# A second level of Strassen's block products in a fused attention block: q, k and the projection with 49 products in place of 56, their weights streamed from DRAM

## The chip, the cores and the metric

One Trainium2 chip, one of its cores. The metric is the device time of one launch in microseconds (us). A kernel is run several times; the median is quoted. Ratios and their 95% intervals are computed from fast runs against runs of the kernel before in the same rounds on the same chip. Every run used here is fast, with a mean granted TensorE clock between 0.988 and 0.999 of full.

Names of engines in the profile: PE is TensorE's matmuls, PEld its weight loads, DVE is VectorE, ACT is ScalarE, POOL is GpSimd, SP is SyncE, which issues most transfers here. SBUF is the memory on the core, PSUM the banks in which TensorE accumulates.

## The reference, cut to what matters

For each of 16 images of 512 channels and 32 x 32 = 1024 positions, in fp32: group normalisation, attention with 4 heads of 128 channels, a projection, and the residual.

```python
def _L0_conv_ref(x, norm_gamma, norm_beta, qkv_w, qkv_b, proj_w, proj_b):
    xg = x.reshape(b, NUM_GROUPS, -1)                      # b = 16, NUM_GROUPS = 8
    xn = ((xg - mu) * jax.lax.rsqrt(var + EPS)).reshape(b, c, h, w)
    xn = xn * norm_gamma[:, None, None] + norm_beta[:, None, None]
    qkv = jnp.einsum('oc,bchw->bohw', qkv_w, xn) + qkv_b[:, None, None]
    q, k, v = jnp.split(qkv, 3, axis=1)                    # then to 4 heads
    attn = jax.nn.softmax(jnp.einsum('bhnd,bhmd->bhnm', q, k) * scale, axis=-1)
    out = jnp.einsum('bhnm,bhmd->bhnd', attn, v)           # back to b, c, h, w
    out = jnp.einsum('oc,bchw->bohw', proj_w, out) + proj_b[:, None, None]
    return x + out
```

## The kernel before

It already uses one level of Strassen's scheme (in Winograd's form, with few additions): the q/k, v and projection products are cut into 2 x 2 blocks, and 7 block products replace 8. TensorE does the seven; the sums of weight blocks (`s1` to `s4`) are made once; the sums of data blocks (`t1` to `t4`) and the recombination of the seven results are made for each image, most of them on VectorE.

```python
FACTORS = {     # product: (weight block or sum, data block or sum)
    1: ("a11", "b11"), 2: ("a12", "b21"), 3: ("s4", "b22"), 4: ("a22", "t4"),
    5: ("s1", "t1"), 6: ("s2", "t2"), 7: ("s3", "t3"),
}

def quad(name, mm, results, order=(1, 6, 2, 7, 5, 4, 3), home=None):
    # bank(i): one of TWO PSUM banks that rotate under one tag
    def p1():
        mm(bank(1), 1, True)
        u["p1"] = upool.tile(...)
        nc.scalar.copy(u["p1"], banks[1])
    def p6():
        mm(bank(6), 6, True)
        nc.vector.tensor_add(u[2], banks[6], u["p1"])
    def p2():
        mm(banks[1], 2, False)           # accumulates onto product 1
        results["c11"](banks[1])
    ...                                  # p7, p5, p4, p3 in the same way

# q/k of one head: mm is two matmuls (k = 0, 1) of 512 columns
# projection, residual and bias; `eng` is GpSimd here, res[...] holds x:
def add(u, *places):
    for at in places:
        eng.tensor_add(res[at], res[at], u)         # both inputs in SBUF
def put(which, half):
    ...
    nc.vector.scalar_tensor_tensor(t, acc, bias, t, ALU.add, ALU.add)   # acc in PSUM
```

Attention runs in 512 steps (16 images x 4 heads x 8 blocks of 128 positions). In each, TensorE makes a block of scores (two matmuls of 512 columns in the program, 4 instructions in the trace: 2048 over the 512 steps), ScalarE its exponentials `p`, VectorE adds them to `tot`, and TensorE the weighted sum of the step before into `po`. Products are spread over the steps as "units", issued between a step's scores and the weighted sum:

```python
for s in range(steps + 1):
    if s < steps:
        b, h, j = where(s)
        if j == 0:
            plan = plan_head(b, h)       # which products run beside this head
        scores(s)
        if j == 2 and s > NB:
            divide(*where(s - NB)[:2])
        for u in plan[j]:
            u()
    if s > 0:
        if s % NB == 0:
            denominators(*where(s - 1)[:2])
        weighted_sum(s - 1)              # po: one PSUM tile; ScalarE copies it to o after 8
```

The compiler then orders the instructions of each engine.

## Time and profile before

| | before |
|---|---|
| time, median of the fast runs | 3372.2 us |
| first to last `tot` transpose (64, one per head), "the stretch" | 3234.7 us |
| from the last of them to the end | 38.4 us |
| one image in the steady state (mean of images 1 to 14) | 208.3 us |
| of this, TensorE not streaming columns | 2.1 us |

The stretch is read from the source view of the transposes, which gives the first and the last start. It is one line per kernel:

```profile
L491 DVE STREAM_TRANSPOSE tt<-tot x64: 1232/1236/1246, 95.7 to 3330.4; 128x1024 f32<-128x1024 f32 x64
```

The last row of the table is a count of mine over the trace: start of each matmul to start of the next, less the time that its columns take at the constant rate that the prediction reads (0.429 us for 512 columns, half of it for 256). Recounts from the packed traces give 1.9 to 2.3 us here, according to how narrow matmuls are priced, so differences of a few tenths in such counts mean little. I use the count because the page's busy share hides losses: ends of matmuls are modelled. A matmul alone is recorded with 0.38 us where its 256 columns take 0.216, and a gap inside a group counts as busy. The rest of the profile before is in the prediction.

### The profile page before, as it was taken

To read this page: it belongs to the slowest core of one execution; us is meant where nothing else is said; L and a number is where in the kernel's file an instruction comes from. 1 tells how busy PE (TensorE), PEld (TensorE's weight loads), DVE (VectorE), ACT (ScalarE), POOL (GpSimd) and SP (SyncE) were. 2 spreads that over 40 slices of the span, in tenths; PEclk is the share of its full clock that TensorE was granted. 3 is DMA by queue.
4 is the path that set the end of the run, shared out by engine and by line. 5 is a ranking of instruction groups with operands and counts; after the bars stand their busy time and mean duration, and the time that the engine had idled before them with its cause. 6 is when DMAs were issued, how large, how long until landed. Compare 5 with 4: busy or idle time off the path is not lost. (4 is left out here: it accounts for less than half of the span.)

```text
span 3368.8 us, 23014 instructions
## 1 busy us (share of the span) xinstructions
PE 3334.8 (99%) x8692; PEld 1634.4 (49%) x8692; DVE 1632.5 (48%) x2454; ACT 790.7 (23%) x870; POOL 141.9 (4%) x110
## 2 busy tenths in 40 slices
PE   8999999999999999999999999999999999999998
PEld 5454454544545445454544545445454454544543
DVE  5553544535445364544545445454454534545444
ACT  2221212212222122221222222221222212222121
POOL 0000000000000000000000000000000000000000
PEclk9999999999999999999999999999999999999999
DMA  2101111011110111101111010110101101011011
GB/s 75 38 21 48 38 41 53 25 44 38 46 48 26 44 38 50 44 25 44 38 53 41 25 50 32 53 41 26 50 31 57 38 25 50 32 60 41 25 44 63
DMA packets 63813, 140.25 MB, mean 42 GB/s; under 512 B 10448, under 2 KB 14544, under 8 KB 63696
## 3 DMA queue, kind: packets, MB, share of 16 engines
q1 hardware_dynamic: 62688, 137.66, 12.0%
q8 instruction: 70, 1.15, 0.1%
q10 hardware_dynamic: 1008, 1.06, 0.1%
q14 instruction: 47, 0.39, 0.0%
HBM read 104.87 MB, written 33.82 MB: 41 GB/s over the span
## 5 line engine op out<-in xcount | busy, mean ns | idle before, releaser
L479 ACT ACTIVATE p<-s 128x1024 f32<-128x1024 f32 x512 | 522.6, 1024 | 2054.3 <-PE s L474 2049.6
L518 PE MATMUL po<-p,v 128*128 128x512 f32 x2048 | 976.5, 594 | 0.0
L474 PE MATMUL s<-qk,qk 128*128 128x512 f32 x2048 | 962.3, 592 | 0.0
L484 DVE TENSOR_TENSOR tot<-tot,p 128x1024 f32<-128x1024 f32 x384 | 470.1, 1224 | 920.5 <-ACT p L479 920.0
L474 PEld LDWEIGHTS s<-qk,qk 128*128 128x128 f32 x2048 | 389.1, 190 | 489.4 <-issue 474.8
L518 PEld LDWEIGHTS po<-p,v 128*128 128x128 f32 x2048 | 385.4, 190 | 453.5 <-issue 393.0
L351 PE MATMUL qk<-xt,wqk_a 128*128 128x512 f32 x512 | 242.5, 596 | 6.3 <-DVE qk_u L315 5.5
L351 PE MATMUL qk<-x,wqk_s 128*128 128x512 f32 x512 | 243.3, 593 | 2.2 <-DVE qk L368 2.2
L351 PE MATMUL qk<-x,wqk_a 128*128 128x512 f32 x512 | 242.2, 595 | 0.0
L527 DVE TENSOR_TENSOR o<-o,rinv 128x1024 f32<-128x1024 f32 x64 | 78.4, 1225 | 244.5 <-ACT o L524 128.7
L439 POOL TENSOR_TENSOR y<-y,pp_u 128x512 f32<-128x512 f32 x90 | 112.7, 1266 | 1882.6 <-DVE pp_u L315 1758.5
L351 PEld LDWEIGHTS qk<-xt,wqk_a 128*128 128x128 f32 x512 | 95.9, 190 | 133.9 <-issue 114.1
L351 PEld LDWEIGHTS qk<-x,wqk_s 128*128 128x128 f32 x512 | 97.0, 190 | 125.8 <-issue 116.1
L351 PEld LDWEIGHTS qk<-x,wqk_a 128*128 128x128 f32 x512 | 95.9, 190 | 126.7 <-issue 106.7
L445 DVE SCALAR_TENSOR_TENSOR y<-pp,projb_sb,y 128x512 f32<-128x512 f32 x124 | 92.7, 748 | 120.6 <-PE pp L418 99.8
L368 DVE SCALAR_TENSOR_TENSOR qk<-qk,qkb_sb,qk_u 128x512 f32<-128x512 f32 x192 | 142.0, 746 | 11.5 <-PE qk L351 11.4
L351 PE MATMUL qk<-xt,wqk_s 128*128 128x512 f32 x256 | 120.6, 593 | 2.0 <-DMA wqk_a<-in_qkv_wT 2.0
L384 PE MATMUL v<-wv_a,xt 128*128 128x256 f32 x512 | 120.9, 379 | 0.0
L384 PE MATMUL v<-wv_s,x 128*128 128x256 f32 x512 | 120.9, 379 | 0.0
L384 PE MATMUL v<-wv_a,x 128*128 128x256 f32 x512 | 120.9, 379 | 0.0
L418 PE MATMUL pp<-ot,wp_a 128*128 128x512 f32 x248 | 118.4, 599 | 0.8 <-DVE pp_u L325 0.8
L418 PE MATMUL pp<-o,wp_a 128*128 128x512 f32 x248 | 118.1, 598 | 1.0 <-DVE o L527 1.0
(104 smaller groups left out, 2062.7 us busy)
## 6 DMA issues: line engine op xcount, KB each, us to landing
rinv<-row SPq DMA_DIRECT2D x64, 512.0 KB, 3.6
y<-in_x SPq DMA_DIRECT2D x128, 256.0 KB, 2.8
out_y<-y SPq DMA_DIRECT2D x128, 256.0 KB, 2.0
x<-in_x SPq DMA_DIRECT2D x62, 512.0 KB, 3.8
wqk_a<-in_qkv_wT SPq DMA_DIRECT2D x8, 192.0 KB, 4.5
x<-in_x ACTq DMA_DIRECT2D x2, 512.0 KB, 6.8
wv_a<-in_qkv_wT SPq DMA_DIRECT2D x8, 128.0 KB, 2.9
wp_a<-in_proj_wT SPq DMA_DIRECT2D x8, 128.0 KB, 3.4
```

Of the source, the lines that this page charges most:

```text
L351: nc.tensor.matmul(acc, wqk[wn][k][:, ts(h, P)], xb[b][xn][k], start=(first and k == 0), stop=(k == KC - 1), skip_group_check=True,)
L368: return lambda acc, u: nc.vector.scalar_tensor_tensor(dst(which, half), acc, bias(which), u, ALU.add, ALU.add)
L384: nc.tensor.matmul(acc[:, ts(g, HC)], xb[b][xn][k][:, ts(2 * jj + g, P)], wv[wn][k], start=(first and g == 0 and k == 0), stop=(k == KC - ...
L418: nc.tensor.matmul(acc, wp[wn][k][:, ts(o, P)], ob[b][on][k], start=(first and k == 0), stop=(k == KC - 1), skip_group_check=True,)
L439: eng.tensor_add(res[at], res[at], u)
L445: nc.vector.scalar_tensor_tensor(t, acc, bias, t, ALU.add, ALU.add)
L474: nc.tensor.matmul(sc[:, ts(half, HALF)], ks[b, h][:, ts(j, P)], qs[b, h][:, ts(half, HALF)], start=True, stop=True,)
L479: nc.scalar.activation(ps[s], sc, AF.Exp, scale=SCALE)
L484: nc.vector.tensor_add(tot[b, h], tot[b, h], ps[s])
L518: nc.tensor.matmul(po[b, h][:, ts(half, HALF)], vs[b, h // 2][:, h % 2, j, :], p[:, ts(half, HALF)], start=(j == 0), stop=(j == NB - 1),)
L527: nc.vector.tensor_mul(os_[b, h], os_[b, h], rinv.pop((b, h)))
```

## The change

**Intent.** Apply the scheme a second time to each of the seven products of q and k (two heads at once, a "pair") and of the projection: 7 x 7 = 49 quarter-size products replace 7 x 8 = 56. TensorE has 12.5% fewer columns there. What it needs:

- Matmuls have 256 columns in place of 512, grouped so that two outer products share a bank's tile of 512 columns (`OUTER`).
- The weight sums of both levels are no longer held in SBUF. They are made for the first image, kept in DRAM, and streamed in 0.9 MB blocks, group by group.
- Each group needs inner data sums of 256 columns, evictions into `R`, and outer sums: all on VectorE and ScalarE.
- A group has one bank x and one bank y, in place of two banks that rotate.
- The normalisation of images 1 to 15 becomes two ScalarE passes; half of it was on VectorE.
- The residual adds of the projection stay on GpSimd: eight per image in place of six, one in front of each final add.

The core of the diff; the first launch's weight staging, the start, the end and the v part are cut:

```diff
+OUTER = ((1, 5), (2, 6), (7, 4), (3,))
+ORDER = (1, 2, 6, 5, 7, 4, 3)
...
-    ps_a = ctx.enter_context(tc.tile_pool(name="ps_a", bufs=2, space=bass.MemoryType.PSUM))
+    ps_a = ctx.enter_context(tc.tile_pool(name="ps_a", bufs=1, space=PSUM))
...
     def normalise(b, c, half=None):
         t = xs[b, c] if half is None else xs[b, c][:, ts(half, HALF)]
-        norm.apply(t, t, *scaled[b], c, True)
+        mu, sc, nmu = scaled[b]
+        if nmu is None:
+            norm.apply(t, t, mu, sc, c, True)
+        else:
+            i = slice(c, c + 1)
+            nc.scalar.activation(t, t, AF.Identity, bias=nmu[:, i])
+            nc.scalar.activation(t, t, AF.Identity, bias=beta_sb[:, i], scale=sc[:, i])
...
+    def group_weights(site, g, first):
+        group = OUTER[g]
+        w = wpool.tile([P, 2, 7, P], F32, tag="w", name=f"w_{site}_{g}")
+        if not first:
+            nc.sync.dma_start(w[:, : len(group)], store[site, g])
+            return w
...
+    def strassen(name, mm, out_, spare=False, width=HALF):
+        def bank(which):                      # which is "x" or "y"
+            return ps_a.tile([P, HALF], F32, tag=which, name=f"{name}_{which}")
+        def kept_copy(n):
+            nc.scalar.copy(t[n][:, :width], t["x"][:, :width])
+        def p1():
+            t["x"] = bank("x")
+            mm(t["x"], 1, True)
+            kept_copy("p1")
+        def p2():
+            t["y"] = bank("y")
+            mm(t["y"], 2, True)
+            out_("c11", t["y"], t["p1"])      # VectorE empties y
+        def p6():
+            mm(t["x"], 6, False)
+            kept_copy("u2")                   # ScalarE copies x
+        def p5():
+            t["y"] = bank("y")
+            mm(t["y"], 5, True)
...
+                for i, p in enumerate(group):        # the inner sums
+                    def put(o, a, c):
+                        nc.vector.tensor_sub(have[o][:, i, :], inner(i, a), inner(i, c))
+                    put("t1", "b12", "b11")
+                    put("t2", "b22", "t1")
+                    put("t3", "t2", "b11")
+                    put("t4", "b21", "t2")
...
+        def combine(g):                              # the outer sums
+            if g == 1:
+                finish("c11", part(0, 0), part(1, 0))
+                nc.vector.tensor_add(part(1, 1), part(0, 0), part(1, 1))
+                nc.vector.tensor_add(part(1, 0), part(1, 1), part(0, 1))
+            elif g == 2:
+                nc.vector.tensor_add(part(2, 0), part(1, 1), part(2, 0))
+                finish("c21", part(2, 0), part(2, 1))
+                finish("c22", part(2, 0), part(0, 1))
+            elif g == 3:
+                finish("c12", part(1, 0), part(3, 0))
...
+    def proj_groups(b, eng, **kw):
+        def finish(which, a, c):
+            for r in range(2):
+                ...                                  # t: residual x, loaded by DMA
+                eng.tensor_add(c[:, r, :], c[:, r, :], t)
+                nc.vector.scalar_tensor_tensor(
+                    t, a[:, r, :], projb_sb[:, o : o + 1], c[:, r, :], ALU.add, ALU.add
+                )
...
-            spread(plan, qk_units(b, 1), 0, NB)
+            spread(plan, sum(qk_groups(b, 1), []), 0, NB)
...
+                spread(plan, sum(proj_groups(b - 1, nc.gpsimd), []), 0, NB)
```

## The prediction

> **What bounds the kernel now.** I read the page first (busy shares, slices), then the groups by line, the timeline of single batches, and the chain that ended last.
>
> ```profile
> PE 3334.8 (99%) x8692; PEld 1634.4 (49%) x8692; DVE 1632.5 (48%) x2454; ACT 790.7 (23%) x870; POOL 141.9 (4%) x110
> PE   8999999999999999999999999999999999999998
> PEclk9999999999999999999999999999999999999999
> ```
> TensorE is busy 99% and its clock is full; no other engine passes half. Busy time alone does not prove that PE is at its own limit, so I read the spacing of matmuls in the timeline of one batch (start, length, work):
>
> ```profile
> 2930.36 1.88 PE L518 MATMUL po<-p,v 128*128 128x512 f32 x4
> 2932.07 1.88 PE L474 MATMUL s<-qk,qk 128*128 128x512 f32 x4
> 2933.79 1.89 PE L384 MATMUL v<-wv_a,x 128*128 128x256 f32 x8
> 2935.52 1.89 PE L384 MATMUL v<-wv_s,xt 128*128 128x256 f32 x8
> ```
> Starts are 1.71 to 1.73 us apart, whether the block is 4 instructions of 512 columns or 8 of 256: 0.429 us per 512 columns, 0.216 us per 256. So PE streams at a constant rate per column, and narrow matmuls cost nothing extra: the weight load (190 ns by its rows) hides behind a 216 ns matmul. Each fp32 matmul is two instructions. The end of the trace is a real chain: the last attention sum ends near 3331 us, the division waits for its denominators, and the projection follows.
>
> ```profile
> 3336.13 4.90 DMA rinv<-row
> 3341.13 1.24 DVE o L527
> ```
> Before kernel outside the steady state: PE starts at about 17 us and is the bound from about 21; after the last sum 37 us pass for 24 us of projection work. In between PE loses almost nothing (204.6 of 205 us busy between 1000 and 1205 us).
>
> [...] The change gives each group only one bank x and one bank y; no run yet shows what that costs. [...] Here 0.5 MB x loads land after 3.8 us[...].
>
> **The change, part by part.**
>
> *PE, removed.* Per batch, q and k have now 4 heads x 7 products x 2 halves of the contraction x 2 instructions = 112 of 512 columns (1792 over 16 batches, as counted): 112 x 0.4293 = 48.1 us. After: two pairs x 49 products x 2 instructions = 196 of 256 columns: 196 x 0.2159 = 42.3 us. The projection goes from 56 x 0.4293 = 24.0 to 98 x 0.2159 = 21.2 us. The v products stay one-level. Saved 5.8 + 2.9 = 8.6 us per batch, 138 us in 16. If all else hides: 3372 - 138 = **3234 us**, 4.1% less. That is the ceiling on the gain.
>
> *DVE, added.* The rows used:
>
> ```profile
> L315 DVE TENSOR_TENSOR qk_u<-qk,qk_p 128x512 f32<-128x512 f32 x64 | 43.3, 676 | 44.0 <-PE qk L351 44.0
> L368 DVE SCALAR_TENSOR_TENSOR qk<-qk,qkb_sb,qk_u 128x512 f32<-128x512 f32 x192 | 142.0, 746 | 11.5 <-PE qk L351 11.4
> L484 DVE TENSOR_TENSOR tot<-tot,p 128x1024 f32<-128x1024 f32 x384 | 470.1, 1224 | 920.5 <-ACT p L479 920.0
> L149 DVE TENSOR_TENSOR wv_s<-wv_s,wv_a 128x256 f32<-128x256 f32 x2 | 0.8, 414 | 0.0
> L310 ACT COPY qk_p<-qk 128x512 f32<-128x512 f32 x64 | 37.5, 586 | 83.0 <-PE qk L351 83.0
> ```
> One two-level site (a pair's q and k, or one projection) needs 7 x 4 inner sums of 256 columns, 28 x 0.414 = 11.6 us; 9 evictions of 512 columns and 3 of 256, 9 x 0.69 + 3 x 0.42 = 7.5; 3 outer adds of 1024 columns, 3.7; and, for q and k, 8 final adds with bias, 8 x 0.746 = 6.0. So 28.8 us per pair, 22.8 for the projection (its 8 final adds exist already): 80.4 us per batch, 1286 us in all, and perhaps 16 net for the weight sums done once. Removed: the u2 and u3 adds (175.7 us), the q/k bias adds (142.0) and the normalisation's DVE half for 15 batches (44.8): 362. DVE goes from 1632 to about **2570 us, 79% of the span**. Back to back, DVE instructions start closer together than they last (two 512-column sums in 1.28 us on the timeline, 1.21 us from one such pair to the next), so real room is larger than it looks.
>
> By head: PE needs 27.5 us of attention plus 21.2 us of units, 48.7 us (51 in the v head); DVE needs 13.6 for attention sums, denominators and division. Head 0 (28.8 + 13.6 + 5.4 for sums of o) is 47.8, head 1 (22.8 + 6.0 + 13.6 + 7.3 for statistics) 49.7, head 2 23, head 3 42.4. With the back-to-back rate, heads 0 and 1 come to some 42 to 44: close to PE, below it.
>
> *ACT.* Four copies per group in place of one per quad, 8.6 us per site at 586 ns and less for the short group, 4.7 for v; normalisation becomes two passes, 8 x 1.09 us in one burst at the end of head 1. From 791 to about 1210 us, 37%.
>
> *Banks.* A group is p1,p2,p6,p5,p7,p4,p3, of 0.86 us each. Bank x must be copied out by ACT (0.59 us and some 0.3 us of signalling on both sides, as read off the timeline) between p1,p6,p7,p4; bank y by DVE between p2,p5,p3. The other bank's product covers most of it: unbroken, a group takes about 7.2 us for 6.05 us of work, and 6.9 us of attention per group lies free to fill the gaps. The compiler's order does fill gaps already: where the sums of x delay q/k at the start of head 3, it pulls two blocks of scores together, and PE loses one small gap:
>
> ```profile
> 2889.95 3.60 PE L474 MATMUL s<-qk,qk 128*128 128x512 f32 x8
> 2901.86 1.98 PE L351 MATMUL qk<-xt,wqk_a 128*128 128x512 f32 x4 [0.36 <-DVE qk_u L315]
> ```
> Not every gap will be filled: outer adds and next inner sums form DVE bursts of 6 to 7 us between groups, and the ACT burst of 8.7 us holds exponentials and copies together. **I choose 2.4 us lost per batch, 36 us**; that is judged, not computed: about 0.2 us for each of 12 to 14 groups.
>
> *DMA, added.* 49 blocks of 64 KB x 3 sites and 2 x 1.8 MB for v, 13 MB per batch, some 205 MB; with the 138 MB of now about 105 GB/s. A group's 0.9 MB [...] against a 12 us group with two buffers: hidden, except perhaps around v, whose loads cover 3, 3 and 1 products.
>
> *Start and end.* The start must finish both heads of pair 0 before the first scores: beside 21 us of PE lie some 24 to 30 us of DVE that cannot be done earlier, plus first weight sums: +12 us of idle PE. The end: after the division, DVE has 1.8 + 6.7 + 4.6 + 3.4 + 10 = about 26 us of sums, evictions and final adds, where PE has 15; the previous end took 26 us from the division to the last add. I add 9 us to the ideal.
>
> Sum: 3234 + 12 + 9 + 36 = 3291, so **3290 us**, 2.4% faster.
>
> **The rivals.**
> *A: DVE hides nearly everywhere.* For: the average is 79% by length and below 75% by spacing, and the compiler's order filled gaps before. Steady loss near nothing, 3234 + 21 = about 3255 us.
> *B: DVE becomes the bound in heads 0 and 1, with the single banks passing each delay on to PE.* For: 47.8 and 49.7 us of DVE by lengths against 48.7 of PE, [...]adds on GpSimd (1.27 us each) in front of final adds. Against: the room in head 2. A loss of 6 to 9 us per batch, 3345 to 3390 us: the gain is gone.
> *C: weights arrive late.* For: a load waits in one queue with residual loads, stores and denominators, and can only start when a buffer is freed. Against: 12% DMA share now and 12 us per group. If 2 us per group were exposed, 12 groups, 24 us per batch, it would be slower by 7%; I give it 3%.
> *D: narrow matmuls expose weight loads.* The v rows speak against it: 216 ns each with loads of 190 ns.
>
> **Range and chances.** Between A and the mild form of B lies 3240 to 3345; I take that as the 80% range. 2% faster is 3304.8 us: the steady loss may then be 3.3 us per batch, against 2.4 chosen. Hence faster 0.60, same 0.35, slower 0.05.
>
> **What would show it.** Right: q/k and projection matmuls of 256 columns spaced 0.216 us; PE busy near 3200 us with 97 to 98% of the span; DVE near 2550 us, ACT near 1200; PE's idle time in front of q/k and projection matmuls released by DVE or ACT, each below 1 us; DMA over 100 GB/s but hardly ever a releaser. Wrong: PE below 95%, with long waits for DVE after outer adds (B), for weight loads (C), or exponentials held by normalisation at the turn from head 1 to 2. The prediction is also wrong below 3245 us if start and end overlap more than I allow.

## The result, and the profile after

The changed kernel is correct and takes **3431.18 us** (median of 4 fast runs, 3427.11 to 3434.47) against 3372.26 in the same rounds: ratio 1.0174, interval 1.0156 to 1.0192. It is 1.7% slower where I had predicted 2.4% faster. It lies outside my range of 3240 to 3345. A ratio here is the mean time of one kernel's fast runs over that of the other's of the same rounds, so it is not quite the ratio of the medians quoted.

Page of the changed kernel, busy times and slices:

```profile
PE 3282.7 (96%) x10708; PEld 1985.4 (58%) x10708; DVE 2473.8 (72%) x4305; ACT 1172.2 (34%) x1602; POOL 190.9 (6%) x140
PE   7999999999999999999999999999999999999997
DVE  8858577675776858668586785867758677586776
```

The instruction count follows from the prediction's numbers of products: 8692 - 1792 - 896 + 196 x 16 + 98 x 16 = 10708. VectorE and ScalarE are close to my 2570 and 1210. PE is still "busy" for 96%, and one could take that for a kernel at TensorE's limit. But PE's busy time fell by 52 us only, where the columns fell by 138, and its idle time rose from 34 us (3368.8 - 3334.8) to 145.

The stretch, from the source view of the changed kernel:

```profile
L638 DVE STREAM_TRANSPOSE tt<-tot x64: 1233/1234/1246, 120.5 to 3376.9; 128x1024 f32<-128x1024 f32 x64
```

I split the time into start, stretch and end, and compare each with what it would be if the change lost nothing. Work also moves: before, the q/k products of heads 0 and 1 of the first image (12.0 us each) lay ahead of the first transpose. Now those of two pairs do (21.2 us each), so 18.3 us of the stretch's work moved to the start. The projection of the last image became 2.9 us shorter at the end.

| part | before | lossless after the change | measured after | lost | predicted loss |
|---|---|---|---|---|---|
| start, to the first transpose | 95.7 | 95.7 + 18.3 = 114.0 | 120.5 | 6.5 | 12 |
| stretch | 3234.7 | 3234.7 - 138.4 - 18.3 + 2.9 = 3080.9 | 3256.4 | **175.5** | **36** |
| end | 38.4 | 38.4 - 2.9 = 35.5 | 50.5 | 15.0 | 9 |

Start and end together lost 21.5 us, against 21 predicted. The whole miss is in the steady state. An image takes 211.6 us, where 208.3 - 8.6 = 199.7 were to be had: 11.9 us lost per image, against the 2.4 that I chose. In my count over the trace, TensorE's gaps grew from 2.1 to 14.3 us per image. By head they are 2.75, 5.02, 4.96 and 1.59 us, where before they were 0.27, 0.26, 0.37 and 1.19.

What do the gaps wait for? The waits view of PE before,

```profile
PE qk L351 <- DVE qk_u L315: 5.5, 15, 0.4
PE pp L418 <- DVE pp_u L325: 0.8, 1, 0.8
```

and after (us in total, times, longest):

```profile
PE pp_y L483 <- DVE pp_r L498: 44.8, 32, 1.9
PE qk_y L483 <- DVE qk_r L498: 18.6, 40, 1.4
PE po L665 <- ACT o L671: 15.0, 14, 1.1
PE v_x L561 <- ACT x L232: 14.8, 28, 0.6
PE pv L60 <- DVE vv L58: 12.0, 15, 1.2
...
PE v_x L561 <- DMA w_v<-kept_v: 3.9, 12, 0.4
```

So TensorE waits for VectorE to empty bank y, above all in the projection (head 1), and at the turn to head 2 for ScalarE, which normalises the next image. Streamed weights hardly appear. These waits sum to 109 us. The gaps contain more: each time a wait is ended late, the matmul behind it starts late too (a "late weight load" below), which is taken up in the part on why the prediction was wrong.

**Why is bank y emptied so late, when VectorE is busy only 72%?** The timeline of the changed kernel (start, length, work):

```profile
1617.70 0.69 DVE L498 TENSOR_TENSOR pp_r<-pp_y,pp_u 128x512 f32<-128x512 f32 x1 [0.89 <-PE pp_y L483]
...
1618.47 1.27 POOL L602 TENSOR_TENSOR pp_r<-pp_r,y 128x512 f32<-128x512 f32 x1 [0.53 <-DVE pp_r L498]
1618.50 2.32 DVE L514 TENSOR_TENSOR pp_r<-pp_r,pp_r 128x1024 f32<-128x1024 f32 x1
```

The outer sum on VectorE starts 0.03 us after GpSimd's residual add and lasts 2.32 us, in place of the 1.22 that a sum of this size takes. The difference is near the length of the GpSimd add. The groups by line (count | total us, mean ns of one | idle just before, and what ended it) show it all over this head. After:

```profile
L603 DVE SCALAR_TENSOR_TENSOR y<-pp_r,projb_sb,pp_r 128x512 f32<-128x512 f32 x94 | 83.4, 902 | 25.8 <-POOL pp_r L602 25.7
L468 DVE TENSOR_TENSOR pp_t<-ot,pp_t 128x256 f32<-128x256 f32 x94 | 52.9, 576 | 0.0
L514 DVE TENSOR_TENSOR pp_r<-pp_r,pp_r 128x1024 f32<-128x1024 f32 x16 | 36.0, 2251 | 1.6
```

The mean of such an outer sum is 2251 ns and of an inner sum 576, where the same shapes for q and k, away from GpSimd, have 1225 and 412 to 420. Before the change GpSimd made such adds too, yet nothing was held. Timeline of before:

```profile
907.87 2.49 POOL L439 TENSOR_TENSOR y<-y,pp_u 128x512 f32<-128x512 f32 x2 [104.03 <-DVE pp_u L315]
907.96 0.75 DVE L368 SCALAR_TENSOR_TENSOR qk<-qk,qkb_sb,qk_u 128x512 f32<-128x512 f32 x1 [0.17 <-PE qk L351]
...
909.87 0.69 DVE L325 TENSOR_TENSOR pp_u<-pp,pp_u 128x512 f32<-128x512 f32 x1 [1.16 <-PE pp L418]
```

Two VectorE instructions lie beside GpSimd adds at their usual 0.75 and 0.69 us. The difference is where they read: these take one operand from a PSUM bank (`qk`, `pp`) and one from SBUF. The held ones take both from SBUF. In my count over both traces this divides them, save where VectorE's instruction starts first. Beside a GpSimd add, the 1024-column sum of L514 has 2320 ns and 1215 alone, a final add (L603) 1735 and 744, inner sums up to 1530 and some 415. L498, which reads PSUM, has 691 and 683. The clearest exception is the 1024-column sum of L511, with both operands in SBUF as well: it starts before the add and keeps 1225 ns, and it is the add that takes 2.31 us in place of 1.27 (15 such pairs, one per image but the last):

```profile
335.58 1.23 DVE L511 TENSOR_TENSOR pp_r<-pp_r,pp_r 128x1024 f32<-128x1024 f32 x1
335.62 2.31 POOL L602 TENSOR_TENSOR pp_r<-pp_r,y 128x512 f32<-128x512 f32 x1 [1.62 <-DVE pp_r L498]
```

So the trace has the hold in both orders of start: where GpSimd's add starts first, VectorE's sum goes from 1215 to 2320 ns (L514), and where VectorE's starts first, the add goes from 1.27 to 2.31 us (L511). What in the chip brings it about is not shown. The hold summed over the changed kernel is some 70 us of VectorE time in my count, and it falls in head 1, where bank y waits.

The second place, head 1 to head 2, in the timeline after:

```profile
1633.02 3.23 ACT L231 ACTIVATE x<-x,nmu 128x1024 f32<-128x1024 f32 x3 [1.14 <-DVE nmu L221]
...
1637.03 3.51 ACT L232 ACTIVATE x<-x,beta_sb,sc 128x1024 f32<-128x1024 f32 x3 [0.79 <-DVE sc L66]
...
1641.48 0.99 ACT L671 COPY o<-po 128x1024 f32<-128x1024 f32 x1
...
1642.53 1.98 PE L665 MATMUL po<-p,v 128*128 128x512 f32 x4 [1.07 <-ACT o L671]
```

ScalarE runs seven of its eight passes first, and the copy of the finished head's `po` stands behind them: the last matmul into that `po` was over at about 1632.5, and the copy began 9 us later. The next head's weighted sum waits for that copy, as `po` has one tile.

### The profile page after: what moved, and what is told of

Same layout as the page of the kernel before. It is cut to its first block, busy times and chain, and to the rows that moved or that the text cites. A ratio compares the mean times of both kernels' runs of the same rounds, so it can differ in the third digit from the quotient of the medians.

```text
span 3427.4 us, 30729 instructions
## 1 busy us (share of the span) xinstructions
PE 3282.7 (96%) x10708; PEld 1985.4 (58%) x10708; DVE 2473.8 (72%) x4305; ACT 1172.2 (34%) x1602; POOL 190.9 (6%) x140
## 3 DMA queue, kind: packets, MB, share of 16 engines
q1 hardware_dynamic: 112848, 354.27, 30.8%
## 4 chain that ended last, share of the span: by engine, by line
PE 70%; DVE 12%; DMA 11%; ACT 3%; issue 2%; POOL 2%; SPq 1%; POOLq 0%; ACTq 0%; DVEq 0%
PE po L665 19%; PE s L621 18%; PE qk_x L483 9%; PE qk_y L483 7%; PE v_x L561 5%; PE pp_x L483 4%; PE v_y L561 4%; DMA rinv<-row 3%; DMA w_v<-kept_v 3%; PE pp_y L483 3%; DVE y L603 2%; DVE tot L631 2%; POOL pp_r L602 2%; ACT x L232 1%; DMA y<-in_x 1%
## 5 line engine op out<-in xcount | busy, mean ns | idle before, releaser
L483 PE MATMUL qk_x<-qk_t,w 128*128 128x256 f32 x1326 | 364.6, 391 | 0.3 <-ACT qk_u L398 0.3
L483 PEld LDWEIGHTS qk_x<-qk_t,w 128*128 128x128 f32 x1326 | 238.3, 189 | 176.0 <-ACT qk_u L398 79.3
L602 POOL TENSOR_TENSOR pp_r<-pp_r,y 128x512 f32<-128x512 f32 x120 | 173.0, 1451 | 2927.0 <-ACT pp_r L496 2686.4
L498 DVE TENSOR_TENSOR qk_r<-qk_y,qk_u 128x512 f32<-128x512 f32 x252 | 156.0, 619 | 46.0 <-PE qk_y L483 45.8
L483 PE MATMUL pp_x<-pp_t,w_proj 128*128 128x256 f32 x654 | 181.8, 395 | 0.0
L561 PE MATMUL v_y<-w_v,x 128*128 128x256 f32 x720 | 172.4, 379 | 0.0
L561 PE MATMUL v_x<-w_v,xt 128*128 128x256 f32 x720 | 171.4, 381 | 0.0
L561 PEld LDWEIGHTS v_y<-w_v,x 128*128 128x128 f32 x720 | 136.7, 190 | 49.8 <-issue 28.1
L483 PE MATMUL qk_y<-x,w 128*128 128x256 f32 x504 | 143.8, 387 | 15.3 <-DVE qk_r L498 14.5
L532 DVE SCALAR_TENSOR_TENSOR qk<-qk_r,qkb_sb,qk_r 128x512 f32<-128x512 f32 x190 | 136.3, 746 | 1.1
```

Of the source, the lines that this page charges most:

```text
L483: nc.tensor.matmul(acc[:, ts(i, Q)], have["w"][:, i, SLOTS[an], :], inner(i, bn), start=(first and i == 0), stop=True, skip_group_check=True,)
L498: nc.vector.tensor_add(dst, view(a), view(c))
L532: nc.vector.scalar_tensor_tensor(st[b, h][:, ts(half, HALF)], a[:, r, :], qkb_sb[:, i : i + 1], c[:, r, :], ALU.add, ALU.add,)
L561: nc.tensor.matmul(acc[:, ts(g, HC)], xb[b][bn][k][:, ts(2 * jj + g, P)], wi[:, k, :], start=(first and g == 0 and k == 0), stop=(k == KC ...
L602: eng.tensor_add(c[:, r, :], c[:, r, :], t)
```

## The experiments

The theories at stake. **G**: GpSimd's adds hold VectorE, and this delays bank y. **N**: the normalisation on ScalarE delays `v` and `po`. **L**: VectorE simply has too much to do (rival B of the prediction). **W**: weights arrive late (rival C). **M**: narrow matmuls themselves cost time (rival D). **P**: two products stand back to back without attention work between them, so each handoff of a bank (TensorE fills it, another engine empties it, TensorE may use it again) is exposed. Medians are in us; "lost" is the loss in the stretch against the lossless 3080.9, from the profiled run.

| run | median | ratio to before [95%] | stretch | lost |
|---|---|---|---|---|
| after | 3431.18 | 1.0174 [1.0156, 1.0192] | 3256.4 | 175.5 |
| e1: residual adds on VectorE | 3371.38 | 0.9996 [0.9980, 1.0013] | 3195.4 | 114.5 |
| e2: normalisation as before | 3422.02 | 1.0141 [1.0124, 1.0158] | 3248.4 | 167.5 |
| e4: no inner sums (wrong results) | 3400.78 | 1.0081 [1.0064, 1.0098] | 3229.7 | 148.8 |
| e9: no streaming (wrong results) | 3422.48 | 1.0142 [1.0125, 1.0159] | 3252.7 | 171.8 |
| e6: e1 and e2 | 3339.76 | 0.9898 [0.9882, 0.9915] | 3164.4 | 83.5 |
| e7: e1, units split | 3325.88 | 0.9862 [0.9846, 0.9879] | 3151.7 | 70.8 |
| e10: e1, e2, units split | 3300.59 | 0.9787 [0.9771, 0.9803] | 3124.4 | 43.5 |
| e13: e10, no inner sums (wrong results) | 3277.57 | 0.9721 [0.9705, 0.9738] | 3103.9 | 23.0 |
| e11: e1, with unread GpSimd adds | 3472.75 | 1.0300 [1.0283, 1.0317] | 3297.9 | 217.0 |
| e8: e1, projection with one level | 3375.45 | 1.0014 [0.9997, 1.0031] | | |
| e12: e10, last projection one level | 3297.74 | 0.9781 [0.9765, 0.9797] | | |
| e5: before, with narrow matmuls | 3393.73 | 1.0060 [1.0043, 1.0077] | | |

Numbers run to e13; there is no e3. Runs e1, e2, e4 and e5 shared one chip, e6 to e9 another, e10 to e12 a third; e13 ran on a fourth. The medians of the kernel before on the four chips lie between 3372.6 and 3373.1.

### e1: the residual adds on VectorE

```diff
-                spread(plan, sum(proj_groups(b - 1, nc.gpsimd), []), 0, NB)
+                spread(plan, sum(proj_groups(b - 1, nc.vector), []), 0, NB)
```

> The residual adds of the projection go from GpSimd to VectorE, nothing else. Theory G (GpSimd and VectorE block each other in the projection's head): the adds of 1024 columns there fall from 2251 to 1225 ns, the inner sums from 520 to 576 back to about 415, TensorE's waits for the y bank in that head shrink from 3.35 us to under 1.5 us per batch, and the time falls by 20 to 40 us, to about 3400. Theory V (VectorE has simply too much work): 8 more adds of 0.69 us per batch make it worse, by 15 to 40 us, to 3450 to 3470.

Measured: 3371.38 us, 60 us less than after, more than the 20 to 40 that G let expect. VectorE has 120 more instructions, and yet the same busy time: 2472.6 us against 2473.8. The held groups are back to their lengths:

```profile
L603 DVE SCALAR_TENSOR_TENSOR y<-pp_r,projb_sb,pp_r 128x512 f32<-128x512 f32 x94 | 68.5, 745 | 0.1
...
L514 DVE TENSOR_TENSOR pp_r<-pp_r,pp_r 128x1024 f32<-128x1024 f32 x16 | 19.6, 1224 | 0.5
```

and PE's wait in the projection shrank to a fifth:

```profile
PE pp_y L483 <- DVE pp_r L498: 8.5, 22, 0.7
```

What follows: giving VectorE more work made the kernel faster. It fits G and not L. But the edit also removes the wait of the final adds for GpSimd's result (25.7 us in the row above of after), and the compiler's order changed with it, so G needed e11. (TensorE's order differs from after's at 180 of 10708 places, ScalarE's nowhere.)

### e2: the normalisation half on VectorE, as before

```diff
-        if b > 0:
+        if False:
             nmu = gn.tile([P, NCC], F32, tag="nmu", name=f"nmu_{b}")
...
-        if nmu is None:
+        if True:
             norm.apply(t, t, mu, sc, c, True)
```

> The normalisation as in the kernel before: one pass on VectorE, one on ScalarE, in place of two on ScalarE. Theory N (the burst of eight passes on ScalarE holds exponentials and evictions at the turn from head 1 to head 2): the waits of v_x and po for ScalarE, 2.6 us per batch, fall under 1 us and the time falls by 15 to 30 us. Theory V (VectorE has too much work): 3 us more of it per batch cost as much as is won or more, the time stays within 10 us of 3431 or rises.

Measured: 3422.02 us, 9 us less. The wait for the copy of `o` went (15 us), but in the projection the waits stayed at 44.6 us. By head, TensorE's gaps fell by 1.4 us per image in head 2 and grew by 0.7 in head 1. By itself the run decided little about N; e6 did.

### e4: no inner sums (wrong results on purpose)

```diff
-                for i, p in enumerate(group):
-                    def put(o, a, c): ...            # the 256-column sums
...
+                m = {"t1": "b12", "t2": "b22", "t3": "b11", "t4": "b21"}.get(m, m)
```

> Wrong results on purpose: the 28 inner sums of each two-level site are left out and blocks are multiplied in their place, so VectorE loses some 550 us of work while TensorE, ScalarE, the banks and the transfers keep theirs. Theory V: TensorE's idle time above that of the kernel before, 12.2 us per batch, mostly goes; 3431 falls by 110 us or more, to 3320 or less. Theory H (the loss is in the handoffs: one bank each, a wait at nearly every product, the exposed weight load behind it, and the turn of heads): it falls by less than 70 us, and the gaps of 0.1 us behind a wait stay near 37 per batch.

Measured: 3400.78 us. VectorE lost 1344 instructions and 487 us of busy time (2473.8 to 1986.5), and the time fell by only 30 us. This refutes L as the main cause: with VectorE at 58% the stretch still loses 149 of 176 us.

### e5: the kernel before, with 256-column matmuls

```diff
-                nc.tensor.matmul(
-                    acc, wqk[wn][k][:, ts(h, P)], xb[b][xn][k],
-                    start=(first and k == 0), stop=(k == KC - 1), skip_group_check=True,
-                )
+                for q in range(2):
+                    nc.tensor.matmul(
+                        acc[:, ts(q, 256)], wqk[wn][k][:, ts(h, P)], xb[b][xn][k][:, ts(q, 256)],
+                        start=(first and k == 0 and q == 0), stop=(k == KC - 1),
+                        skip_group_check=True,
+                    )
```

and the same for the projection.

> The kernel before, with each matmul of q, k and the projection cut into two of 256 columns: same products, same sums, same waits, twice the weight loads. If narrow matmuls are free, as the prediction had it, 3372 stays within 5 us. If each wait in front of a narrow matmul exposes 0.1 us of a weight load, there are about 56 products a batch with a wait at most of them: 3 to 5 us per batch, 3372 plus 50 to 80 us. If weight loads were not hidden at all, the loss would be over 200 us.

Measured: 3393.73 us, 21 us or 1.4 us per image more, for 168 more matmuls per image. That lies between the first two forecasts. M is real but small: narrowness alone explains at most that much of the 11.9 us. Some 0.4 of the 1.4 us is the spacing itself (168 x (2 x 0.2159 - 0.4293) us), which the prediction had priced. The changed kernel has fewer narrow matmuls for q, k and the projection, 294 per image against 336 here. TensorE's gaps came to 3.5 us per image, with 11 late weight loads as against 10 before.

### e6: e1 and e2 together

The two edits shown above, in one kernel.

> The residual adds on VectorE (as in the first run) and also the normalisation's first pass on VectorE, as before the change. With GpSimd out of the way, the turn from head 1 to head 2 should lose what it lost to ScalarE: the wait of po for the eviction of o (1.24 us per batch) goes and that of v_x halves. Theory N (ScalarE's burst): 3371 falls by 15 to 30 us, to about 3350. If instead VectorE's 3 us of added work per batch cost as much, it stays within 8 us of 3371.

Measured: 3339.76 us, 1% faster than before. On top of e1 the normalisation is worth 32 us (31 in the stretch), where alone it was worth 9. The wait of `po` for `o` is gone, and that of `v_x` for ScalarE, 9.7 us in e1, is no longer in the waits view. So N is shown, but only where the projection's delay in front of it is gone. I did not find out why the two hide each other; one reading, not tested, is that in e2 the four VectorE passes fall into the same crowded end of head 1, where the gaps grew.

### e7: e1, with the weighted sum in the middle of a step's products

```diff
-            run(plan[j])
+            early = (len(plan[j]) + 1) // 2
+            run(plan[j][:early])
         if s > 0:
             if s % NB == 0:
                 denominators(*where(s - 1)[:2])
             weighted_sum(s - 1)
+        if s < steps:
+            run(plan[j][early:])
```

> The first run's kernel (adds on VectorE), with the weighted sum of each step placed in the middle of the step's products in place of behind them, so that each bank has 1.7 us more between a product and its reuse. Theory H (handoffs of the single banks that come late): the late waits, 36 per batch with 3.5 us of exposed weight loads behind them, fall to 25 or fewer, the waits for the y bank shrink, and the time falls by 20 to 50 us from 3371. If the compiler had already put the weighted sums where the gaps are, nothing changes: within 8 us.

Measured: 3325.88 us, 45 us less than e1 and 44 less in the stretch (ratios 0.9996 and 0.9862), with not one instruction added or removed on TensorE. PE's wait for VectorE in q/k fell from 18.8 us in e1 to

```profile
PE qk_y L483 <- DVE qk_r L498: 7.5, 12, 1.4
```

and late weight loads from 36 to 25 per image. This supports P: a block of attention of 1.7 us between the products covers the handoff of a bank. The compiler's order of the other engines changed with the edit (488 of VectorE's 4425 places, 98 of ScalarE's 1602), and what that did by itself is not shown.

### e8: e1, with the projection back to one level

The q and k products keep two levels; the projection uses the one-level scheme, with its own streamed weights.

```diff
-                spread(plan, sum(proj_groups(b - 1, nc.gpsimd), []), 0, NB)
+                spread(plan, proj_units(b - 1, 0, nc.vector) + proj_units(b - 1, 1, nc.vector), 0, NB)
```

> The first run's kernel, but the projection with one level of seven-for-eight, its weights streamed; q and k keep two levels. TensorE has 2.9 us more work per batch. Its idle time in head 1 was 2.1 us per batch above nothing in the first run; so the second level of the projection is worth at most 1 us per batch in the steady state, and costs 14 us at the end of the program. I expect 3371 within 15 us either way: the projection's second level is worth next to nothing, the end gets shorter by 8 to 14 us, the batches longer by 0.5 to 1.5 us. If it falls by over 20 us, the projection's second level was a loss; if it rises by over 30, a real gain.

Measured: 3375.45 us against 3371.38 for e1, with ratios 1.0014 and 0.9997: no difference that the intervals separate. An image takes 207.9 us against 207.3, and the end is 7 us shorter (44.8 against 51.9 us after the last weighted sum). So the second level of the projection, counted at 2.9 us per image, yields 0.6 us: in e1 its gaps in head 1 (some 2.0 us, against 0.2 here) eat the gain.

### e9: no streaming (wrong results on purpose)

```diff
+    def fixed():                      # one weight tile, loaded once, for all groups
...
-        if not first:
-            nc.sync.dma_start(w[:, : len(group)], store[site, g])
-            return w
+        if not first:
+            return fixed()
```

> Wrong results on purpose: the changed kernel as it is, but with one block of weights that stays in the chip's memory, so that the 200 MB of streamed weights are gone. Theory S (streamed weights come late, or their traffic delays the residual loads that GpSimd waits for): 3431 falls by 40 us or more. Otherwise, by the waits for weights that the trace shows (0.4 us per batch, 6 us in all, and some 4 us at the end): 3420, within 8 us.

Measured: 3422.48 us. With no weights streamed at all after the first image the kernel gains 9 us, and 4 in the stretch. W is refuted, although the queue moves 354.27 MB in place of 137.66.

### e10: all three mends

e1, e2 and the split of e7 in one kernel.

> The three mends together: residual adds on VectorE, the normalisation's first pass on VectorE, the weighted sum in the middle of a step's products. If their causes are separate (GpSimd against VectorE in head 1; ScalarE's burst at the turn to head 2; late handoffs of the banks everywhere), the gains add: 3326 less some 30, about 3295, and TensorE's idle time falls to about 5 us per batch. If the added work on VectorE now shows, 3310 or more.

Measured: 3300.59 us, 2.1% faster than before, correct. Whether it is more than 2% is open, as the interval of the ratio (0.9771 to 0.9803) includes 0.98. The three savings add up nearly: 61 (G) + 31 (N) + 44 (P) = 136 us, and e10's stretch is 132 us shorter than that of after. Its page and its waits view:

```profile
PE 3240.3 (98%) x10708; PEld 1996.4 (61%) x10708; DVE 2508.2 (76%) x4470; ACT 1101.8 (33%) x1542; POOL 16.8 (1%) x20
```

```profile
PE qk_y L483 <- DVE qk_r L498: 7.5, 13, 1.3
PE pp_y L483 <- DVE pp_r L498: 6.9, 21, 0.4
```

VectorE's share, 76%, is with that of e12 the highest of the correct kernels, and yet PE waits little. An image takes 202.4 us; the prediction's sum had 208.3 - 8.6 + 2.4 = 202.1. That is no confirmation, as e10 is another kernel than the one predicted.

### e11: e1, with GpSimd adds that nobody reads

Each residual add on VectorE is followed by a GpSimd add of two SBUF blocks into a tile that nothing reads; no instruction waits for it.

```diff
-                eng.tensor_add(c[:, r, :], c[:, r, :], t)
+                added = eng.tensor_add(c[:, r, :], c[:, r, :], t)      # VectorE
+                if b < B - 1:
+                    idle = nc.gpsimd.tensor_add(
+                        scratch, blocks_o[b][r][:, 0:448], blocks_o[b][r][:, 512:960]
+                    )
+                    tc.add_manual_dep(idle.ins, added.ins.name, ...)   # issue it after
```

> The first run's kernel (adds on VectorE, 3371) with 8 adds of 448 columns per batch put on GpSimd beside them, whose results nobody reads and for which nothing waits; the order of instructions on TensorE, VectorE and ScalarE is the same as in the first run. Theory G1 (the two engines hold each other up where VectorE reads two operands from the chip's memory): VectorE's sums in head 1 get longer again, TensorE's waits for the y bank grow from 0.9 to 2 us or more per batch, the time rises by 25 us or more, to 3395 or higher. Theory G2 (the changed kernel lost its time because final adds stood waiting for GpSimd's result): nothing waits here, so 3371 within 8 us.

Measured: 3472.75 us, 101 us more than e1. The order of instructions on TensorE, VectorE and ScalarE is the same as e1's, instruction by instruction, so neither the compiler's order nor a wait for a result can be the reason. VectorE has the same 4425 instructions and 103.5 us more busy time (2576.1 against 2472.6). The timeline shows the hold:

```profile
1621.06 3.52 POOL L608 TENSOR_TENSOR scratch<-o 128x448 bf16<-128x448 f32 x2 [180.09 <-DVE pp_r L606]
...
1621.97 1.63 DVE L618 SCALAR_TENSOR_TENSOR y<-pp_r,projb_sb,pp_r 128x512 f32<-128x512 f32 x1
...
1623.52 2.15 DVE L646 TENSOR_TENSOR tot<-tot,p 128x1024 f32<-128x1024 f32 x1
```

1.63 us in place of 0.75, and 2.15 in place of 1.22. Passed on to PE (e1 had 8.5 us here):

```profile
PE pp_y L487 <- DVE pp_r L502: 66.5, 31, 3.7
```

A recount of the trace finds 107 us of holds: 53 in final adds, 28 in `tot`, and 26 in 28 instructions of the normalisation's statistics, of only 128 x 4 elements: 161 ns alone, 1090 beside a GpSimd add.

This settles that the hold by itself costs time: here it arrives at the end almost one to one, though VectorE is idle a quarter of the time. The holds of e11 fall in part on other instructions than those of after (inner and outer sums there), so e11 shows the mechanism and its price and not how after's 61 us divide.

### e12: e10, with the last image's projection at one level

The end uses `proj_units` of e8 in place of `proj_groups`; all other images keep two levels.

> The three mends together, and the last batch's projection, where nothing runs beside it, with one level in place of two. The end lay 52 us behind the last weighted sums with two levels and 45 with one (first and one-level run), so 7 to 10 us less than the run with the three mends: about 3286, a version faster than the kernel before by 2.5%. If staging the extra weights in the first batch costs as much, no difference.

Measured: 3297.74 us, ratio 0.9781 against e10's 0.9787: the intervals overlap, so a gain in all is not shown. The profiled runs show the end 8.5 us shorter, as expected (45.4 against 53.9 us after the last transpose), and the start 1.2 and the stretch 1.7 us longer. It is the fastest correct kernel, 2.2% faster than before, level with e10.

### e13: e10, without inner sums (wrong results on purpose)

The edits of e10 and e4 in one kernel.

> Wrong results on purpose: the kernel with the three mends (3301), without the 28 inner sums per two-level site, as in the run that left them out of the changed kernel (which fell by 30 us of the 180 it loses in its batches). What is left to lose in the mended kernel is some 2.7 us per batch, 40 us. Theory V (that rest is VectorE's load): 3301 falls by 30 us or more. Theory H (that rest is late handoffs of the single banks and the exposed weight loads behind them): it falls by 15 us or less, and the late waits stay above 15 per batch.

Measured: 3277.57 us. Taking 455 us of VectorE work out of the mended kernel brings 23 us, between the two forecasts (30 or more, 15 or less). Of e10's 43.5 us lost in the stretch, about 20 come from the inner sums, and 23 remain.

## Why the prediction was wrong

**The failing step** is the term "I choose 2.4 us lost per batch, 36 us; that is judged, not computed". It measured 11.9 us per image, 175.5 us in the stretch. What fails in it is the step "6.9 us of attention per group lies free to fill the gaps", with the compiler trusted to fill them, and a VectorE priced as if nothing beside it could lengthen its instructions. The other terms of the sum held:

- *The ceiling of 3234 us.* The instruction count is exact, and the spacing of 0.216 us per 256 columns stays: the groups of four last 1.03 us where the wait came early (timeline line below). So the saving of 138 us was there on TensorE. No run reached it; e13, with wrong results, comes within 23 us in the stretch.
- *Start and end.* 12 + 9 predicted, 6.5 + 15.0 measured. The split was off, one term too high and one too low by 6 us; that the sum was right is luck.
- *The loads of the engines.* VectorE 2570 predicted, 2474 measured; ScalarE 1210 and 1172; 205 MB added and 354.27 - 137.66 = 217 measured, at the predicted rate (104 against 105 GB/s). A block of 896 KB landed in 4.7 us (median).
- *Range and chances.* 3431 lies 86 us above the range. I gave 0.05 to slower by over 2% and 0.35 to within 2%; it is within 2% by a little. Of my signs of being wrong, "PE below 95%" did not come (96%), while the waits, said to stay below 1 us each, reached 1.9.

What the 175.5 us are, from the runs:

1. **GpSimd's adds, 61 us** (after to e1). They cost by the hold, some 70 us of VectorE time, and perhaps by the final adds' wait of 25.7 us for their results; e1 removes both. e11 shows that the hold by itself can cost as much (101 us there). In the prediction I priced GpSimd's adds at their own 1.27 us "in front of final adds" and never asked which memories their neighbours read. The profile before held the answer only in part: GpSimd's adds were there, 90 of them, but beside VectorE work that read PSUM. The change put outer sums, inner sums and final adds beside them, with both operands in SBUF.
2. **Single banks without cover, 44 us** (e1 to e7, with the compiler's new order in it). The prediction named this ("6.9 us of attention per group lies free to fill the gaps") and trusted the compiler to fill. It had the material and did not place it: two products stood together, then the weighted sum.
3. **The normalisation burst, 31 us** (e1 to e6; by itself, in e2, 8 in the stretch). I had listed it under what would prove me wrong, and gave it no term in the sum.
4. **The rest, 43.5 us**. That it is close to my 36 is chance, as it is what three mends leave. About 20 belong to the inner sums (e13). The four parts sum to 179.5: the savings, measured in this order, do not add up exactly.

**Rival A** (nothing is lost) is out: even e10 loses 43.5 us. **Rival B** named the right heads, sizes and even GpSimd's adds, but for a wrong reason. VectorE is not the bound in the sense of its load: e4 takes 487 us from it and gains 30, e1 gives it 120 instructions and gains 60. It is late at particular moments, and the single banks pass that on. **Rival C** is refuted by e9 (9 us in all). **Rival D** is real in e5, at 1.4 us per image for 168 matmuls, and small.

One part of the gaps was in no term. Where a wait in front of a matmul is ended late, the next matmul comes 0.105 us late too. The timeline of after, two groups of four:

```profile
1592.29 1.13 PE L483 MATMUL pp_x<-pp_t,w_proj 128*128 128x256 f32 x4
...
1594.11 1.03 PE L483 MATMUL pp_y<-pp_t,w_proj 128*128 128x256 f32 x4
```

The first group was released late by ScalarE's copy and lasts 0.10 us longer. The trace shows that its weight loads were not made ahead: as a rule (9227 of 10708 loads) the next load starts 0.002 us after a matmul's start, and in these cases 0.107 us after it, 0.108 us behind the load before; the load rows of the profile say 190 ns for one. In the count such gaps (some 0.07 to 0.125 us) are 10 per image before, 38 after, 36 in e1, 25 in e7 and 24 in e10: 0.9, 3.9, 3.6, 2.5 and 2.4 us per image. They follow the number of late handoffs and not the narrowness, as e5 has 11.

What stays open: the last 23 us of e13's stretch, 1.5 us per image, of which late weight loads are the largest part; why e2 alone gave 9 us and with e1 31; and how much of e7's gain is the place of the weighted sum itself, as the compiler reordered other engines with it.

## What to carry to other kernels

Before an elementwise step is put on GpSimd or left there, list the VectorE instructions that will lie beside it and mark those with both operands in SBUF: those were held here for about the length of GpSimd's instruction (a sum of 1.22 us took 2.32 beside an add of 1.27), and in this kernel with single PSUM banks that arrived at TensorE, however idle VectorE looked: in e11, 120 unread adds, 188 us of GpSimd time, cost 103.5 us of VectorE time and 101 us of the kernel's. When a change turns rotating banks into single ones, do not price its handoffs with "the scheduler will fill them"; place independent work between two uses of a bank, and measure that placement (44 us of 3371 here, e1 to e7). And judge a TensorE-bound kernel by the spacing of matmul starts over a steady period, as a busy share of 96% hid a loss of 12 us in 212.
